# Raw scores leave PSUM on ScalarE, and the key norm is folded with a small product and applied two slots later

## The chip, the cores and the metric

The kernel runs on one core of a Trainium2 chip. Five engines work side by side, each through its own list of instructions in order: TensorE (PE, with its weight loads PEld), VectorE (DVE), ScalarE (ACT), GpSimd (POOL) and SyncE (SP). TensorE writes to PSUM only; ScalarE and VectorE read PSUM and SBUF. Transfers are issued from SP's and ACT's lists. The metric is the time of one execution on the device in microseconds (us). Before the change it is 2100.78 us, the median of two runs (2096.07 and 2105.5).

## What is computed

Eight batches of 64 tokens of width 512 pass one layer: a cross and self attention of 8 groups of heads, a second attention with a learned sparse mask, and a feed-forward network. The change lies in the cross attention of the tokens to 1601 context rows per batch. Cut to that part:

```python
# per batch b and group g (8 groups, two query heads each: 128 query rows), d = 128
kx, vx = split(cond @ w_kv_x.T)              # keys and values of the 1601 context rows
kx = _ln(kx, kxln_w, kxln_b)                 # layer norm of each key over its 128 features
qx = _ln(fp8_linear(ln_out, wqx), qxln_w, qxln_b)
scores = einsum('bsghd,btgd->bghst', qx, kx) / sqrt(128)
p = softmax(scores)                          # over the 1601 rows
out = einsum('bghst,btgd->bsghd', p, vx)
```

The mean of a key is taken out of the weights ahead of time. The scale, one over the root of the key's variance plus 1e-5, is one number for each key and group. Since it is common to all features of a key, it can multiply the finished scores: score = (query times unscaled key) times scale(key), plus a constant of the query.

## The kernel before, in words

The cross attention is cut into 16 passes (class `Cross`): 8 batches times 2 halves of 4 groups. A pass goes over 13 tiles of 128 context rows (`TT`). The tiles are grouped in six chunks (`CHUNKS`), five of two tiles (256 rows) and a last one of three (321 rows). Keys of a chunk are made two groups at a time (one at a time in part of the last chunk); scores are made, normed and turned into probabilities by chunk; probabilities are transposed and used tile by tile.

One loop over g issues the work of all passes as a pipeline: in step (slot) g, tile g is read and split, tile g-2 (`KEYS`) becomes keys, and so on. There are 208 slots and a tail. Keys, queries and probabilities are split into a high and a low part, and each product of two split numbers takes three products on TensorE.

- `keys` (L569 to L599): 12 products per group into a PSUM bank (L585). ACT squares the bank (L592) and copies it, scaled, to the high part `kthi` (L593); DVE transposes the squares in blocks of 32 (L595), takes the low part `ktlo` (L596) and adds up the squares (L597). The result `kms` holds, on each of 128 partitions, sums over parts of the features: feature sums still lie on four blocks of 32 partitions.
- `norm` (L601 to L617), at the end of the slot in which a chunk's last keys are made: DVE copies the four blocks beside each other (L609, four copies on 32 partitions), adds them for each group (L611, four reductions), POOL raises to the power -0.5 (L613), DVE transposes (L615), and SP writes the row of scales to `keyd` in device memory (L617).
- `spread` (L619 to L623), two slots later: an ACT-issued transfer reads the row back into a tile `S`, broadcast to all 128 partitions, 512 KB.
- `scores` (L625 to L649), three slots after the keys (`SCORES` 5 against `KEYS` 2): TensorE makes the scores into one of three PSUM banks of a pool (`mainp`), which keys, scores and transposed probabilities share. DVE multiplies each group's scores by the scales in `S`, writes the product over them in `S` and keeps the maximum (L646). For the last chunk, DVE also copies the query's constant (L649).
- `maxima` and `exps`: after a pass's last chunk, the row maximum, and exponentials on ACT in place in `S` (L662). `S` has eight buffers.
- `probs_t`, `weigh`: 15 or more slots later the probabilities are transposed by TensorE (L674), split by ACT and DVE (L684, L685), and multiplied with the context (L737 to L739).

Beside the passes run generators (`bgA`, `bgB`, `bgC`) at a set pace: projections, the self attention, the output products (L440), the second attention (`attn`, L804 on) and the preparation of the feed-forward weights. The feed-forward network itself ends the program.

A planner fixes each engine's order of instructions ahead of time. It gives preference to what stands earlier in the program, among what its own clock holds to be ready. `tc.issue_after(x)` only puts an instruction behind x on its engine. At run time an engine that waits holds up all that stands behind it, and a transfer issued from ACT's list waits there for its data.

Of the kernel before, what the change touches and what calls it, by code (L numbers as in the profile page):

```python
# [11 lines left out]
F32 = mybir.dt.float32  # L12
F32R = mybir.dt.float32r
# [8 lines left out]
P = 128  # L22
# [19 lines left out]
LAG = 20  # L42
KEYS, SPREAD, SCORES = 2, 4, 5
ALL = 10 ** 6
# [17 lines left out]
def tile_perceiver(ctx: ExitStack, tc: tile.TileContext, t: dict):  # L62
# [168 lines left out]
    for h in range(2):  # L231
        V.tensor_copy(fold[h * S:(h + 1) * S], ident[h * S:(h + 1) * S, h * S:(h + 1) * S])
    spread = [ctile([P, 32], F32, f"spread{i}") for i in range(2)]
    parts = [ctile([32, HG * NRM, 5], F32, f"parts{i}") for i in range(2)]
    for x, y in zip(spread, parts):
        V.memset(x, 0.0)
        V.memset(y, EPS)
    mhalf = ctile([P, NRM], F32, "mhalf")
# [63 lines left out]
    def projection(v_, blocks, js, first=None):  # L302
# [17 lines left out]
        for nb in blocks:  # L320
# [17 lines left out]
            for i0 in range(0, len(js), 2):  # L338
# [14 lines left out]
                if v_ == "v":  # L353
# [5 lines left out]
                    continue  # L359
                st = sm("hst", 24)  # L360
                ag = sm("hag", 8)
# [168 lines left out]
    class Cross:  # L530


        def __init__(self, b, half):
            self.b, self.half = b, half
            self.raw = None
            self.S = {}
            self.kt = {}
            self.ct = {}
            self.ms = {}
            self.qb = sm("cqb", HG, bufs=2)  # L540
# [60 lines left out]
        def norm(self, ci):  # L601

            cw = sum(TT[tt][1] for tt in CHUNKS[ci])
            nj = (cw + 31) // 32
            ms = self.ms.pop(ci)
            x = parts[ci % 2]
            r = spread[ci % 2]
            for i in range(4):
                V.tensor_copy(x[:, :HG * nj, i], ms[i * 32:(i + 1) * 32, :HG * nj])  # L609
            for g in range(HG):  # L610
                V.tensor_reduce(r[g * 32:(g + 1) * 32, :nj], x[:, g * nj:(g + 1) * nj], AX.X, ALU.add)  # L611
            with tc.issue_after(low[0].ins):
                GP.tensor_tensor(r[:, :nj], r[:, :nj], mhalf[:, :nj], ALU.pow)  # L613
            rt = sm("krt", 32, bufs=2)
            V.transpose(rt, r)  # L615
            rd = keyd[(self.b + self.half * NB) % 2][ci]
            nc.sync.dma_start(rd.rearrange("g (x a) -> (g x) a", a=32), rt)  # L617

        def spread(self, ci):  # L619

            cw = sum(TT[tt][1] for tt in CHUNKS[ci])
            self.S[ci] = mp.tile([P, HG, KTW], F32, tag="S", name=nm("S"), bufs=SB)
            nc.scalar.dma_start(self.S[ci][:, :, :cw], keyd[(self.b + self.half * NB) % 2][ci][:, :cw].partition_broadcast(P))  # L623

        def scores(self, ci):  # L625
            chunk = CHUNKS[ci]
            cw = sum(TT[tt][1] for tt in chunk)
            hi, lo = self.kt.pop(ci)
            N = cw + (cw & 1)
            if N > cw:  # L630

                for x, y in ((hi, kbhi), (lo, kblo)):
                    gp_copy(x[:, :, cw:N], y.bitcast(F32).unsqueeze(2))
            sc = self.S[ci]
            per = 512 // N
            for g0 in range(0, HG, per):
                bank = mainp("s")
                gs = range(g0, g0 + per)

                for k, (a, x) in enumerate(((self.qhi, hi), (self.qlo, hi), (self.qhi, lo))):  # L640
                    for i, g in enumerate(gs):
                        PE.matmul(bank[:, i * N:(i + 1) * N], lhsT=a[:, g * P:(g + 1) * P], rhs=x[:, g, :N],  # L642
                                  start=k == 0 and i == 0, stop=k == 2, skip_group_check=True)
                for i, g in enumerate(gs):
                    ps = bank[:, i * N:(i + 1) * N]
                    V.tensor_tensor_reduce(sc[:, g, :cw], ps[:, :cw], sc[:, g, :cw], 1.0, -3.0e38,  # L646
                                           ALU.mult, ALU.max, self.mx[:, g * NCH + ci:g * NCH + ci + 1])
                    if N > cw:
                        V.tensor_copy(self.qb[:, g:g + 1], ps[:, cw:N])  # L649

        def maxima(self):

            top = sm("ctop", HG)
            V.tensor_reduce(top, v3(self.mx, HG), AX.X, ALU.max)
            V.tensor_tensor(top, top, self.qb, ALU.add)
            self.nmx = sm("cnm", HG)
            V.tensor_tensor(self.nmx, self.qb, top, ALU.subtract)  # L657

# [38 lines left out]
        def context(self, tt):  # L697
            t0, n = TT[tt]
            if tt == len(TT) - 1:
# [3 lines left out]
                chi = mp.tile([P, 512], F32R, tag="chi", name=nm("chi"), bufs=2)  # L703
                clo = mp.tile([P, 512], F32R, tag="clot", name=nm("clot"), bufs=1)
                A.copy(chi, raw)
# [98 lines left out]
    def attn(j, x, o=0, n=P, kept=False, L=bgl):  # L804
# [92 lines left out]
        else:  # L897
# [3 lines left out]
            V.tensor_scalar(sim[:n], ps[:n, :S], at["b3"][:n], None, ALU.add)  # L901
        for b in range(nb):
            r = slice(b * S, (b + 1) * S)
            GP.affine_select(out=sim[r], in_=sim[r], compare_op=ALU.not_equal, fill=0.0, base=0,
                             pattern=[[-1, S]], channel_multiplier=1)
        yield
# [16 lines left out]
        for k0, k1 in ((0, 4), (4, KSEL)):  # L923
            w = (k1 - k0) * P
            sel = fa()
            GP.memset(sel, 0.0)
            for b in range(nb):
# [78 lines left out]
    def ffn_rows(pairs, kind):  # L1006

        if kind == 0:
            z2 = ph.tile([P, 2, NIC, 256], F32R, tag="ws", name=nm("z2"), bufs=1)
            rows = ph.tile([P, 2, 512], F32, tag="cats", name=nm("fx"), bufs=1)  # L1010
            ac["ffn_b2"] = bcast_row(mp.tile([P, 512], F32, tag="sq", name=nm("b2"), bufs=1), t["ffn_b2"])
        else:
# [192 lines left out]
    for g in range(NA + LAG + 3):  # L1205
# [26 lines left out]
        if 0 <= g - SPREAD < NA and LAST[kN]:  # L1232
            with tc.issue_after(turn[0].ins):
                work[nN].spread(JOBS[kN][0])
        if 0 <= g - SCORES < NA:
            nS, kS = divmod(g - SCORES, NT)
            ci = CHUNK_OF[kS]
            w = work[nS]
            if kS == CHUNKS[ci][-1]:
                if ci == 0:  # L1240
                    w.queries()
                w.scores(ci)
                if ci == NCH - 1:
                    w.maxima()
                    w.exps(0, 0, 2)
        if g == LAG - 4:
# [18 lines left out]
        if g == TERNARY_AT:  # L1265
            bgB.add(ternary("ffn_w1", w1t), ternary("ffn_w2", w2t))
        if 0 <= g - SCORES - 1 < NA and (g - SCORES - 1) % NT == NT - 1:
            work[(g - SCORES - 1) // NT].exps(0, 2, 4)
        e = g - LAG
# [113 lines left out]
```

## Time and profile before

| quantity | value |
|---|---|
| median of the runs | 2100.78 us (2096.07 and 2105.5) |
| the profiled execution | 2105.96 us, of which the span of its instructions is 2104.2 us |
| PE busy | 1903.1 us, 90% of the span |
| DVE busy | 1501.6 us, 71% |
| ACT busy | 1097.7 us, 52% |
| POOL busy | 557.7 us, 27% |
| transfers | 406.33 MB, 193 GB/s on the mean |
| granted TensorE clock | 0.96 on the mean |

A group of instructions is written as line, engine, operation, output <- inputs, size and count, then busy time and mean duration, then the idle time of the engine just ahead of them with what ended it. A line of the waits gives who waited for whom, the total in us, how often, and the longest. TensorE's products overlap each other, so the mean duration of one (0.28 us for 256 columns) is longer than the distance between two starts.

### The profile page before, as it was taken

Reading aid. Unit: us, or ns where it says so; the run is one execution under the profiler, and the core shown is the slowest. Engines: PE = TensorE matmul, PEld = TensorE weight load, DVE = VectorE, ACT = ScalarE, POOL = GpSimd, SP = SyncE. Lnnn points to the kernel's source line nnn. Section 1 sums busy time; section 2 is a strip of 40 time slices with the busy share of each in tenths; the row PEclk is TensorE's granted clock in tenths of the full one; section 3 lists DMA queues with packets and bytes.
Section 4 is the critical chain, followed back from the end, with each engine's and each line's share of the span. In section 5 each row is a group of like instructions: output and inputs, shape, how many; then the busy total and the mean of one; then the engine's idle time right before and its main releaser. Section 6 shows DMA issues by size and latency. Waiting matters only on the chain.

```text
span 2104.2 us, 36122 instructions
## 1 busy us (share of the span) xinstructions
PE 1903.1 (90%) x11989; PEld 1657.8 (79%) x11989; DVE 1501.6 (71%) x4339; ACT 1097.7 (52%) x2628; POOL 557.7 (27%) x487
## 2 busy tenths in 40 slices
PE   5679998999999899899999999899999999846997
PEld 5568897898988889798888889798887787524766
DVE  7768787878888868977776766576667667534565
ACT  6446654665665555654454444444456545413554
POOL 4332323322323223222222222222223222000132
PEclk9889999999999999999999999999999999958999
DMA  6546565577666567567868777676784665521424
GB/s 197 158 124 186 170 181 159 175 224 241 198 173 189 176 206 229 172 209 235 301 224 260 253 249 244 227 257 209 229 292 128 180 195 165 181 97 62 145 76 150
DMA packets 361036, 406.33 MB, mean 193 GB/s; under 512 B 45696, under 2 KB 255744, under 8 KB 360848
## 3 DMA queue, kind: packets, MB, share of 16 engines
q1 hardware_dynamic: 310160, 351.54, 51.8%
q10 hardware_dynamic: 50688, 52.47, 10.1%
q8 instruction: 95, 1.56, 0.3%
q14 instruction: 93, 0.76, 0.1%
HBM read 336.40 MB, written 67.26 MB: 192 GB/s over the span
## 4 chain that ended last, share of the span: by engine, by line
PE 59%; DMA 18%; DVE 12%; ACT 4%; issue 4%; POOL 1%; SPq 1%; ACTq 0%; POOLq 0%; DVEq 0%
PE kx L585 20%; PE acc L738 5%; PE acc L737 5%; PE acc L739 5%; DMA S<-keyd 5%; DMA ws<-wpd 5%; PE s L642 4%; PE pt L674 3%; PE pp L440 3%; PE pj L349 3%; PE xo L758 2%; PE p L866 2%; DMA keyd<-krt 1%; DMA wv<-in_wkv 1%; DVE S L646 1%
## 5 line engine op out<-in xcount | busy, mean ns | idle before, releaser
L567 POOL TENSOR_TENSOR cTlo<-cTr,cThi 128x512 fp32r<-128x512 f32 (+1 forms) x208 | 247.5, 1191 | 732.3 <-ACT cThi L566 668.0
L738 PE MATMUL acc<-plo,chi 128*128 128x512 f32 x768 | 308.0, 403 | 0.9 <-DVE plo L685 0.9
L739 PE MATMUL acc<-phi,clo 128*128 128x512 f32 x768 | 302.6, 397 | 0.0
L592 ACT ACTIVATE ksq<-kx 128x512 f32<-128x512 f32 (+1 forms) x224 | 123.9, 553 | 340.9 <-PE kx L585 312.0
L585 PE MATMUL kx<-cThi,wkhi 128*128 128x256 f32 (+1 forms) x1536 | 271.6, 297 | 29.7 <-ACT cThi L566 11.6
L585 PEld LDWEIGHTS kx<-cThi,wkhi 128*128 128x128 f32 x1536 | 226.2, 193 | 52.3 <-ACT cThi L566 13.8
L595 DVE STREAM_TRANSPOSE ksqt<-ksq 128x512 f32<-128x512 f32 (+1 forms) x224 | 147.3, 658 | 165.3 <-ACT ksq L592 164.4
L585 PE MATMUL kx<-cTlo,wkhi 128*128 128x256 f32 (+1 forms) x1536 | 261.6, 290 | 0.6 <-POOL cTlo L567 0.6
L585 PE MATMUL kx<-cThi,wklo 128*128 128x256 f32 (+1 forms) x1536 | 259.8, 290 | 0.0
L613 POOL TENSOR_TENSOR spread<-spread,mhalf 128x8 f32<-128x8 f32 x96 | 171.6, 1787 | 325.9 <-DVE spread L611 310.8
L737 PE MATMUL acc<-phi,chi 128*128 128x512 f32 x768 | 247.9, 409 | 2.0 <-ACT phi L684 1.7
L646 DVE CUSTOM_DVE_ANT_0 S<-s,S 128x256 f32<-128x256 f32 (+1 forms) x384 | 152.6, 429 | 105.3 <-DMA S<-keyd 80.3
L585 PEld LDWEIGHTS kx<-cTlo,wkhi 128*128 128x128 f32 x1536 | 220.9, 191 | 5.8 <-issue 2.4
L585 PEld LDWEIGHTS kx<-cThi,wklo 128*128 128x128 f32 x1536 | 221.6, 193 | 4.4 <-issue 4.1
L662 ACT ACTIVATE S<-S,cnm 128x256 f32<-128x256 f32 (+1 forms) x384 | 197.7, 524 | 45.6 <-DVE cnm L657 45.5
L714 ACT CAST chi<-cr 128x512 fp32r<-128x512 f32 x192 | 119.6, 623 | 117.5 <-PE acc L738 64.5
L738 PEld LDWEIGHTS acc<-plo,chi 128*128 128x128 f32 x768 | 147.0, 192 | 27.0 <-issue 2.0
L739 PEld LDWEIGHTS acc<-phi,clo 128*128 128x128 f32 x768 | 145.7, 190 | 26.7 <-issue 1.6
L737 PEld LDWEIGHTS acc<-phi,chi 128*128 128x128 f32 x768 | 139.4, 192 | 26.4 <-ACT phi L684 3.5
L674 PE MATMUL pt<-ident,S 128*128 128x128 f32 (+1 forms) x832 | 138.7, 277 | 20.3 <-ACT S L662 10.3
L685 DVE TENSOR_TENSOR plo<-pt,phi 128x512 fp32r<-128x512 f32 x192 | 130.9, 682 | 30.4 <-ACT phi L684 29.5
L596 DVE SCALAR_TENSOR_TENSOR ktlo<-kx,cols,kthi 128x512 fp32r<-128x512 f32 (+1 forms) x224 | 147.8, 660 | 0.0
(347 smaller groups left out, 3696.4 us busy)
## 6 DMA issues: line engine op xcount, KB each, us to landing
cTr<-in_ctxT SPq DMA_DIRECT2D x192, 256.0 KB
cr<-in_ctx SPq DMA_DIRECT2D x192, 256.0 KB
ws<-wpd SPq DMA_DIRECT2D x88, 512.0 KB
S<-keyd ACTq DMA_DIRECT2D x80, 512.0 KB
clod<-clo SPq DMA_DIRECT2D x96, 256.0 KB
clo<-clod SPq DMA_DIRECT2D x96, 256.0 KB
wv<-in_wkv SPq DMA_DIRECT2D x64, 256.0 KB
tern<-in_ffn_w SPq DMA_DIRECT2D x64, 256.0 KB
```

The source lines that it names most:

```text
L567: low[0] = GP.tensor_tensor(clo[:, :, o:o + n], raw[:, :, :n], chi[:, :, o:o + n].bitcast(F32), ALU.subtract)
L585: PE.matmul(ps[:, i * N:(i + 1) * N], lhsT=st[:, ic, g * P:(g + 1) * P], rhs=mv[:, ic, :N], start=k == 0, stop=k == 11)
L595: V.transpose(sqt[:, :ng * W], sq[:, :ng * W])
L596: V.scalar_tensor_tensor(lo[:, g0:g1, :N], v3(ps[:, :ng * N], ng), hw["kx"], hi[:, g0:g1, :N].bitcast(F32), ALU.mult, ALU.subtract)
L613: GP.tensor_tensor(r[:, :nj], r[:, :nj], mhalf[:, :nj], ALU.pow)
L646: V.tensor_tensor_reduce(sc[:, g, :cw], ps[:, :cw], sc[:, g, :cw], 1.0, -3.0e38, ALU.mult, ALU.max, self.mx[:, g * NCH + ci:g * NCH + ci + 1])
L662: A.activation(self.S[ci][:, g, :cw], self.S[ci][:, g, :cw], AF.Exp, bias=self.nmx[:, g:g + 1], accum_out=self.su[:, g * NCH + ci:g * NCH ...
L674: PE.transpose(pt[:n, g * P:(g + 1) * P], self.S[ci][:, g, o:o + n], ident)
L685: V.tensor_tensor(lo[:n], pt[:n], hi[:n].bitcast(F32), ALU.subtract)
L737: PE.matmul(self.U[ic], lhsT=chi[:n, s], rhs=phi[:n], start=tt == 0, stop=False)
L738: PE.matmul(self.U[ic], lhsT=chi[:n, s], rhs=plo[:n], start=False, stop=False)
L739: PE.matmul(self.U[ic], lhsT=clo[:n, s], rhs=phi[:n], start=False, stop=False)
```

## The change

ScalarE copies the raw scores of a whole bank out of PSUM into `S`. VectorE multiplies them in place in a new method `tops`, two slots later, with a tile `row` that the broadcast transfer now fills; `row` has one buffer. The constant of the query is read from `S` and no longer copied. `scores` moves from three slots behind the keys to one slot behind, and takes `norm` with it: `norm` no longer gathers the four blocks of partitions on VectorE but multiplies `kms` with a constant matrix `over` on TensorE (which adds the four blocks and spreads the sums over them), adds 1e-5 and keeps each partition's own group with the mask `quad` in one VectorE instruction, and adds over the groups in a second. The product goes into one more tile of the three-bank pool, behind the last product of the scores. The queries are loaded and split at a pass's first tile. Beside this: the diagonal of the mask's scores is set to zero by a multiplication on VectorE in place of a GpSimd select, a tile is cleared on VectorE in place of GpSimd, the narrow feed-forward weights of the first part load into the two buffers `cTr` in place of the three `raw`, and some buffers are shared or fewer.

```diff
-KEYS, SPREAD, SCORES = 2, 4, 5
+KEYS, SCORES, SPREAD, TOPS = 2, 3, 4, 5
...
+    quad = ctile([P, HG], F32, "quad")
+    for h in range(HG):
+        V.tensor_reduce(quad[:, h:h + 1], ident[:, h * 32:(h + 1) * 32], AX.X, ALU.add)
+    over = ctile([P, P], F32, "over")
+    for h in range(HG):
+        V.tensor_reduce(over[:, h * 32:(h + 1) * 32], ident.rearrange("p (q a) -> p a q", q=HG), AX.X, ALU.add)
...
-    parts = [ctile([32, HG * NRM, 5], F32, f"parts{i}") for i in range(2)]
...
+    off = ctile([P, S], F32, "off")
+    V.tensor_scalar(off, fold, -1.0, 1.0, ALU.mult, ALU.add)
...
-                st = sm("hst", 24)
+                st = sm("hst", 24, bufs=2)
...
         def norm(self, ci):
...
             ms = self.ms.pop(ci)
-            x = parts[ci % 2]
+            z = mainp("kz")
+            with tc.issue_after(self.sm.ins):
+                PE.matmul(z[:, :HG * nj], lhsT=over, rhs=ms[:, :HG * nj], start=True, stop=True)
+            own = sm("kown", HG * NRM, bufs=1)
+            V.scalar_tensor_tensor(v3(own[:, :HG * nj], HG), v3(z[:, :HG * nj], HG), EPS, quad.unsqueeze(2).to_broadcast([P, HG, nj]), ALU.add, ALU.mult)
+            v = sm("kxv", NRM, bufs=2)
+            V.tensor_reduce(v[:, :nj], own[:, :HG * nj].rearrange("p (g j) -> p j g", g=HG), AX.X, ALU.add)
             r = spread[ci % 2]
-            for i in range(4):
-                V.tensor_copy(x[:, :HG * nj, i], ms[i * 32:(i + 1) * 32, :HG * nj])
-            for g in range(HG):
-                V.tensor_reduce(r[g * 32:(g + 1) * 32, :nj], x[:, g * nj:(g + 1) * nj], AX.X, ALU.add)
             with tc.issue_after(low[0].ins):
-                GP.tensor_tensor(r[:, :nj], r[:, :nj], mhalf[:, :nj], ALU.pow)
+                GP.tensor_tensor(r[:, :nj], v[:, :nj], mhalf[:, :nj], ALU.pow)
...
         def spread(self, ci):
...
-            self.S[ci] = mp.tile([P, HG, KTW], F32, tag="S", name=nm("S"), bufs=SB)
-            nc.scalar.dma_start(self.S[ci][:, :, :cw], keyd[(self.b + self.half * NB) % 2][ci][:, :cw].partition_broadcast(P))
+            self.row = mp.tile([P, HG, KTW], F32, tag="row", name=nm("row"), bufs=1)
+            nc.scalar.dma_start(self.row[:, :, :cw], keyd[(self.b + self.half * NB) % 2][ci][:, :cw].partition_broadcast(P))
...
         def scores(self, ci):
...
-            sc = self.S[ci]
+            sc = self.S[ci] = mp.tile([P, HG, KTW], F32, tag="S", name=nm("S"), bufs=SB)
...
-                for i, g in enumerate(gs):
-                    ps = bank[:, i * N:(i + 1) * N]
-                    V.tensor_tensor_reduce(sc[:, g, :cw], ps[:, :cw], sc[:, g, :cw], 1.0, -3.0e38,
-                                           ALU.mult, ALU.max, self.mx[:, g * NCH + ci:g * NCH + ci + 1])
-                    if N > cw:
-                        V.tensor_copy(self.qb[:, g:g + 1], ps[:, cw:N])
+                A.copy(sc[:, g0:g0 + per, :N], v3(bank[:, :per * N], per))
+
+        def tops(self, ci):
+
+            cw = sum(TT[tt][1] for tt in CHUNKS[ci])
+            sc = self.S[ci]
+            for g in range(HG):
+                V.tensor_tensor_reduce(sc[:, g, :cw], sc[:, g, :cw], self.row[:, g, :cw], 1.0, -3.0e38,
+                                       ALU.mult, ALU.max, self.mx[:, g * NCH + ci:g * NCH + ci + 1])
...
-                clo = mp.tile([P, 512], F32R, tag="clot", name=nm("clot"), bufs=1)
+                clo = mp.tile([P, 512], F32R, tag="clo", name=nm("clot"), bufs=2)
...
-        for b in range(nb):
-            r = slice(b * S, (b + 1) * S)
-            GP.affine_select(out=sim[r], in_=sim[r], compare_op=ALU.not_equal, fill=0.0, base=0,
-                             pattern=[[-1, S]], channel_multiplier=1)
+        V.tensor_tensor(sim[:n], sim[:n], off[:n], ALU.mult)
...
-            GP.memset(sel, 0.0)
+            V.memset(sel, 0.0)
...
-            tag, bufs = ("kthi", "ktlo")[k] if kind else "raw", 2 if kind else 3
+            tag, bufs = ("kthi", "ktlo")[k] if kind else "cTr", 2
...
+        nN, kN = divmod(g - TOPS, NT)
+        if 0 <= g - TOPS < NA and LAST[kN]:
+            ci = JOBS[kN][0]
+            w = work[nN]
+            w.tops(ci)
+            if ci == NCH - 1:
+                w.maxima()
+                w.exps(0, 0, 2)
         if 0 <= g - SCORES < NA:
             nS, kS = divmod(g - SCORES, NT)
-            ci = CHUNK_OF[kS]
-            w = work[nS]
-            if kS == CHUNKS[ci][-1]:
-                if ci == 0:
-                    w.queries()
+            if LAST[kS]:
+                ci = JOBS[kS][0]
+                w = work[nS]
                 w.scores(ci)
-                if ci == NCH - 1:
-                    w.maxima()
-                    w.exps(0, 0, 2)
+                w.norm(ci)
+            elif kS == 0:
+                work[nS].queries()
...
-        if 0 <= gK < NA and LAST[kK]:
-            work[nK].norm(JOBS[kK][0])
```

More of the change, by code (lines that the diff above doesn't have):

```diff
@@ L232, in tile_perceiver @@
         V.tensor_copy(fold[h * S:(h + 1) * S], ident[h * S:(h + 1) * S, h * S:(h + 1) * S])
+    quad = ctile([P, HG], F32, "quad")
[4 more added lines that the diff above has]
+        V.tensor_reduce(over[:, h * 32:(h + 1) * 32], ident.rearrange("p (q a) -> p a q", q=HG), AX.X, ALU.add)
     spread = [ctile([P, 32], F32, f"spread{i}") for i in range(2)]
-    parts = [ctile([32, HG * NRM, 5], F32, f"parts{i}") for i in range(2)]
-    for x, y in zip(spread, parts):
+    for x in spread:
         V.memset(x, 0.0)
-        V.memset(y, EPS)
+    off = ctile([P, S], F32, "off")
+    V.tensor_scalar(off, fold, -1.0, 1.0, ALU.mult, ALU.add)
     mhalf = ctile([P, NRM], F32, "mhalf")
@@ L539, in __init__ @@
             self.ms = {}
-            self.qb = sm("cqb", HG, bufs=2)
             self.pp = {}
@@ L641, in scores @@
                     for i, g in enumerate(gs):
-                        PE.matmul(bank[:, i * N:(i + 1) * N], lhsT=a[:, g * P:(g + 1) * P], rhs=x[:, g, :N],
+                        self.sm = PE.matmul(bank[:, i * N:(i + 1) * N], lhsT=a[:, g * P:(g + 1) * P], rhs=x[:, g, :N],
                                   start=k == 0 and i == 0, stop=k == 2, skip_group_check=True)
-                for i, g in enumerate(gs):
-                    ps = bank[:, i * N:(i + 1) * N]
-                    V.tensor_tensor_reduce(sc[:, g, :cw], ps[:, :cw], sc[:, g, :cw], 1.0, -3.0e38,
-                                           ALU.mult, ALU.max, self.mx[:, g * NCH + ci:g * NCH + ci + 1])
-                    if N > cw:
-                        V.tensor_copy(self.qb[:, g:g + 1], ps[:, cw:N])
+                A.copy(sc[:, g0:g0 + per, :N], v3(bank[:, :per * N], per))
[5 more added lines that the diff above has]
+                                       ALU.mult, ALU.max, self.mx[:, g * NCH + ci:g * NCH + ci + 1])
         def maxima(self):
@@ L654, in maxima @@
             V.tensor_reduce(top, v3(self.mx, HG), AX.X, ALU.max)
-            V.tensor_tensor(top, top, self.qb, ALU.add)
+            qb = self.S[NCH - 1][:, :, SC - TT[CHUNKS[-1][0]][0]]
+            V.tensor_tensor(top, top, qb, ALU.add)
             self.nmx = sm("cnm", HG)
-            V.tensor_tensor(self.nmx, self.qb, top, ALU.subtract)
+            V.tensor_tensor(self.nmx, qb, top, ALU.subtract)
         def exps(self, ci, g0=0, g1=HG):
@@ L1010, in ffn_rows @@
             rows = ph.tile([P, 2, 512], F32, tag="cats", name=nm("fx"), bufs=1)
-            ac["ffn_b2"] = bcast_row(mp.tile([P, 512], F32, tag="sq", name=nm("b2"), bufs=1), t["ffn_b2"])
+            ac["ffn_b2"] = bcast_row(mp.tile([P, 512], F32, tag="row", name=nm("b2"), bufs=1), t["ffn_b2"])
         else:
@@ L1266, in tile_perceiver @@
             bgB.add(ternary("ffn_w1", w1t), ternary("ffn_w2", w2t))
-        if 0 <= g - SCORES - 1 < NA and (g - SCORES - 1) % NT == NT - 1:
-            work[(g - SCORES - 1) // NT].exps(0, 2, 4)
+        if 0 <= g - TOPS - 1 < NA and (g - TOPS - 1) % NT == NT - 1:
+            work[(g - TOPS - 1) // NT].exps(0, 2, 4)
         e = g - LAG
```

## The prediction

> **What bounds the kernel now.** I began with busy time by stretches of the span: after the first 200 us TensorE works nearly without rest, VectorE and ScalarE do not (columns: us, then busy time and count of PE, PEld, DVE, ACT, POOL, then granted clock, share and rate of the transfers).
>
> ```profile
> 0.00:200.00 200.00, 141.32 (x942) 132.07 (x943) 154.52 (x484) 103.61 (x243) 72.10 (x70) 0.91 0.57 165
> 400.00:600.00 200.00, 194.70 (x1322) 177.93 (x1320) 166.35 (x511) 127.22 (x320) 64.00 (x53) 1.00 0.69 207
> 1200.00:1400.00 200.00, 189.96 (x1211) 169.68 (x1210) 135.10 (x379) 90.96 (x227) 51.13 (x43) 0.98 0.72 230
> ```
>
> So from 200 to 1800 us a change is worth what it takes from or gives to TensorE's list, plus what it takes from TensorE's waits. I next added up those waits, gap by gap. From 200 to 1800 us they are 72.6 us: 38.8 ended by DVE, 20.1 by transfers, 13.7 by ACT. In the first 200 us they are 58.6 (27.8 DVE, 30.3 ACT), after 1800 us 64.8 (35.4 DVE). DVE is the engine that TensorE waits for most. Then the groups by line, to see which DVE work it is:
>
> ```profile
> L585 PE MATMUL kx<-cThi,wkhi 128*128 128x256 f32 (+1 forms) x1536 | 271.6, 297 | 29.7 <-ACT cThi L566 11.6 <-DVE cmx L646 5.3 <-DVE cqb L649 5.2
> ...
> L646 DVE CUSTOM_DVE_ANT_0 S<-s,S 128x256 f32<-128x256 f32 (+1 forms) x384 | 152.6, 429 | 105.3 <-DMA S<-keyd 80.3 <-PE s L642 21.3 <-PE out L965 1.6
> ...
> L642 PE MATMUL s<-kthi,qxhi 128*128 128x256 f32 (+1 forms) x384 | 92.6, 308 | 22.8 <-DVE cmx L646 8.9 <-DVE cqb L649 5.1 <-ACT cThi L566 5.1
> L609 DVE COPY parts<-kms 32x32 f32<-32x32 f32 (+1 forms) x384 | 79.0, 206 | 4.5
> ...
> L611 DVE TENSOR_REDUCE spread<-parts 32x8 f32<-32x40 f32 (+1 forms) x384 | 71.0, 185 | 4.7
> ```
>
> The reader sees two things. The multiplication of the scores (L646) keeps DVE idle for 80.3 us until the row of scales lands, and all the while a PSUM bank with scores is held: products of keys and scores wait for it. And the fold of the norm is 768 instructions of some 0.2 us, 150.0 us of DVE. Last, the chain of the work that ended last shows what a row costs in latency when it is on the path:
>
> ```profile
> 1240.24 2.11 POOL spread L613
> 1242.61 2.90 DMA keyd<-krt
> 1245.52 11.34 DMA S<-keyd
> ```
>
> Elsewhere in that chain the row's read takes 5.1 to 9 us and its write 2.4 to 4.2.
>
> **The change, part by part.** The sum is made against the profiled execution, 2105.96 us (span 2104.2). It lies 5.2 us (0.25%) above the median 2100.78; I add the same difference to the median.
>
> *Bank released by ACT.* The products that wait for L646 or L649 now wait for an ACT copy. The groups give 5.3 + 5.2 (keys), 8.9 + 5.1 (scores), and 2.7 for the transposes L674: 27.2 us that go. What is late next is ACT. It gains per pass ten copies of 512 columns and four of 322. The copy of 512 columns out of PSUM (L684) takes 0.595 us, L592 on 322 columns 0.443 (by form): 16 x (10 x 0.595 + 4 x 0.443) = 124 us, so ACT goes from 1097.7 to 1222 us, 58%. It lies beside TensorE's work. ACT now makes TensorE wait 58.7 us in the whole span; with 11% more load I give back 6 us. Bounds: nothing, and all 27 if the copy queues as L646 did. Sum -21.
>
> *The fold on TensorE.* 96 products, plain float32. The trace has no product `over` by `kms`. The nearest row is L758, also float32: 256 products have 512 records, two each, and in the chain ten of its records take 1.13 us, 0.11 each. That makes 96 x 2 x 0.11 = 21 us. TensorE is some 5% idle in the middle stretch, so I take +20. Below: 11, if a record of 32 columns costs half of one of 128. Above: 48, at 0.5 us each, if it also stands waiting for `kms`, which DVE finishes (L597, 0.625 us) after `ktlo`, on which the scores just ahead of it depend. A product that waits holds up every product behind it.
>
> *VectorE.* Off go 79.0 + 71.0 of the fold and 9.7 of L649. On come 192 instructions (one out of PSUM, one reduction, 128x32); the nearest rows are L609 and L611 at 0.2 us: 38 us. The 384 multiplications stay and read SBUF; no row shows that form, so I keep 0.43 us, with 0.3 (the distance of two starts is 0.35) and 0.5 as ends: +-40 us of DVE. In all DVE goes from 1501.6 to about 1380 us, 66%. TensorE's other waits for DVE between 200 and 1800 us are 38.8 less 18.0 for L646 and L649, so 21 us. Queueing at 66% in place of 71% is about a fifth shorter (0.66/0.34 = 1.94 against 0.71/0.29 = 2.45): -5. In the first 200 us DVE is 77% busy and the fold of some ten chunks is 16 us of it; TensorE is short of work there, so half of the 12 us saved goes through: -6. Bounds of both together: 0 and -30.
>
> The Trainium skill (VectorE: DVE Perf Modes, Rules for kernel authors) speaks against the detour: on a matmul's output accept the rate out of PSUM, or copy to SBUF first if many operations follow. Here one follows. The same page's table of fixed costs (The TRN2 errata) puts an SBUF source 62 cycles of VectorE below a PSUM source. By that, an estimate, the multiplications would lose 384 x 65 ns = 25 us; by the rule alone the copy would be 124 us for nothing. The rows decide otherwise than the rule only because what it buys is a free bank, not a cheaper operation.
>
> *The row.* Before, from the end of a chunk's last `kms` (medians over 78 chunks, from the starts of the lines) the fold ends at 3.9 us, the write is issued at 6.7, the read at 11.2, the score products start at 16.2 and the multiplication at 19.2. After it, the scores must come first (one slot of 8.7 us behind the keys at most), the fold takes 1 in place of 2.8 us, the multiplication keeps its slot. The row then lands about when it did, with a spread of several us either way. I take 0 for DVE's wait of 80.3 us and treat the rest as a rival. The read is issued from ACT's list; behind it stand the squares, `kthi`, and the copies of probabilities, for which TensorE waits. ACT now idles 27.8 us there, ten times. `row` has one buffer, so the read also waits for the chunk before it to be multiplied, a slot earlier. Value 0, bounds -10 and +30.
>
> *Queries.* They are split on POOL three slots earlier, behind the last scores of the pass before. POOL waited 19.5 us for them in seven cases, TensorE for POOL's `cTlo` 0.6 us in the whole span; POOL is 27% busy, that hides it. Without that cover it is 15 waits of up to 5.7 us.
>
> *The last stretch.* The select and ten clears of 0.52 us leave POOL, where they wait 51.0 + 24.6 us for transfers; DVE gets some 6 us of 154 in 305. DVE waited for that select 7.0 us in all, so the wait moves rather than goes: 0. Weights in two own buffers in place of three shared: ACT and POOL wait 20.5 us for them now; 0. Bounds for both -10 and +10. Shared and fewer buffers elsewhere: 0, no wait names them.
>
> Sum: -21 + 20 - 5 - 6 = -12 us on paper. TensorE also loses time in gaps under 0.15 us that no wait names: between 200 and 1800 us products start about 60 us later in total than at their usual distances. Fewer banks held and a less loaded DVE should take a sixth of it, -10. So -22: 2084 in the profile, **2079** against the median, 1% faster and inside the band.
>
> **The rivals.**
>
> *DVE was the real limit* (faster). For: 102 us of TensorE's idle time end with DVE, and the startup is not bound by TensorE. Against: the fold pays 20 us on the bound engine, and the transfers' 20 us stay. If two thirds of the 102 go, 68, and half of the 60 small ones, 30, against 20 + 6 given back: -72, so 2029 against the median; the case begins at -42, 2059, and its middle is 2044.
>
> *The row comes late* (slower). One mechanism: scores, fold, power, write, read and multiplication now hang one behind the other, within two slots (17.3 us). The parts add up to 0.7 (scores) + 1.5 (fold with its hand-overs) + 1.8 + 0.5 + 2.9 + 6.9 = 14.3 us without any queue. If the planner puts the multiplication 4 us ahead of the landing, DVE stands 96 x 4 = 384 us, and since 101.6 us of waits at L646 cost TensorE 27 us, TensorE loses about a quarter: +100, so 2179. It outweighs the gain from 2.5 us per chunk on (+64 - 22 = +42, 2143). Against: the bank is no longer held meanwhile, so less than a quarter may come through.
>
> *The waits only change their name.* ACT and the fold take back what DVE gave: 2085 to 2110. It is inside the band too.
>
> **How the numbers follow.** A change under 2% (42 us) is about what a measurement of this kernel can't tell from none. Forecast and the third rival together 0.46 (2059 to 2143), faster rival 0.32, late row 0.22. The range reaches into both: 2030 to 2150, which leaves about a tenth out at each end.
>
> **What would show it.** Right: L646 and L649 gone from what keys and scores wait for; the fold's product with two records of 0.11 us distance; DVE near 1380 and ACT near 1220 us; waits of the multiplication for `row` near 80 us. Wrong: those waits above 240 us, scores waiting for `ktlo`, the fold's product waiting for `kms`, or ACT idle over 60 us for `keyd`.

## The result

The changed kernel takes 2222.74 us, the median of two runs (2222.6 and 2222.89), against 2100.78 before: a ratio of 1.0581, with a 95% interval of 1.0478 to 1.0683. The forecast was 2079 us, in a range of 2030 to 2150. The profiled span is 2221.0 us against 2104.2, so 116.8 us more.

The busy times of the changed kernel's page come first (busy us, share of the span, count).

```profile
span 2221.0 us, 35931 instructions
PE 1954.8 (88%) x12181; PEld 1695.3 (76%) x12181; DVE 1389.1 (63%) x3721; ACT 1201.7 (54%) x2852; POOL 549.5 (25%) x469
```

VectorE lost 112.5 us of work and ScalarE took on 104, nearly as worked out. Yet every engine's share but ScalarE's fell, TensorE's from 90% to 88%: something stands more. The same stretches as before, in the same columns (us, then busy time and count of PE, PEld, DVE, ACT, POOL, then granted clock, share and rate of the transfers):

```profile
0.00:200.00 200.00, 142.17 (x953) 131.84 (x954) 136.90 (x420) 111.05 (x258) 71.84 (x68) 0.91 0.56 160
400.00:600.00 200.00, 183.82 (x1202) 165.84 (x1202) 132.04 (x378) 122.95 (x307) 53.32 (x47) 0.97 0.63 195
1200.00:1400.00 200.00, 183.86 (x1186) 163.38 (x1184) 115.57 (x292) 97.13 (x233) 48.38 (x40) 0.99 0.73 232
```

The start is as it was. The loss is in the pipeline of passes: TensorE finishes 1202 products in the second stretch where it finished 1322. The first keys of the last pass begin at 1819 us instead of 1690. These 129 us are the whole loss; what follows gives 12 back. The groups by line name the place (busy us, mean ns of one, then idle time of the engine just ahead and what ended it).

```profile
L590 PE MATMUL kx<-cThi,wkhi 128*128 128x256 f32 (+1 forms) x1536 | 281.1, 304 | 26.7 <-DVE ktlo L601 9.5 <-DVE plo L696 6.9 <-DVE kown L615 6.2
...
L658 DVE CUSTOM_DVE_ANT_0 S<-S,row 128x256 f32<-128x256 f32 (+1 forms) x384 | 163.0, 473 | 295.2 <-DMA row<-keyd 295.2
...
L649 PE MATMUL s<-kthi,qxhi 128*128 128x256 f32 (+1 forms) x384 | 93.4, 311 | 64.6 <-DVE ktlo L601 50.9 <-POOL kthi L521 7.5 <-DVE plo L696 4.6
...
L613 PE MATMUL kz<-kms,over 128*128 128x32 f32 x192 | 33.9, 260 | 12.8 <-DVE plo L696 4.7 <-DVE kms L602 4.3 <-ACT S L651 3.3
```

The multiplication (now L658) keeps VectorE idle for 295.2 us until the row of scales lands; before it was 80.3. It no longer holds a PSUM bank meanwhile: the waits for `cmx` and `cqb` are gone from the lines of keys and scores, as predicted. But the scores (L649) now wait 50.9 us for `ktlo`, the low part of the keys, where the same line waited 22.8 us in all before. The two waits, as us in total, times, and the longest:

```profile
DVE S L658 <- DMA row<-keyd: 295.2, 91, 10.0
...
PE s L649 <- DVE ktlo L601: 64.5, 32, 5.9
```

The second takes all three kinds of score products together. VectorE stands in 91 of 96 chunks. Why that reaches `ktlo` is seen in VectorE's own list. The timeline of VectorE in one slot (start us, us, operation; in brackets the idle time just before and what ended it):

```profile
1179.58 0.42 DVE L658 CUSTOM_DVE_ANT_0 S<-S,row 128x256 f32<-128x256 f32 x1 [5.53 <-DMA row<-keyd]
...
1180.28 0.42 DVE L658 CUSTOM_DVE_ANT_0 S<-S,row 128x256 f32<-128x256 f32 x1
1180.63 0.08 DVE L658 DVE_READ_ACCUMULATOR2_ANT cmx<- 128x1 f32 x1
1180.63 0.75 DVE L601 SCALAR_TENSOR_TENSOR ktlo<-kx,cols,kthi 128x512 fp32r<-128x512 f32 x1
```

VectorE stands 5.53 us for the row, and `ktlo` of a newer tile of keys waits behind. TensorE, at the same time, waits for that `ktlo` before its next scores:

```profile
1181.43 0.51 PE L649 MATMUL s<-kthi,qxhi 128*128 128x256 f32 x2 [2.84 <-DVE ktlo L601]
```

On the chain of the work that ended last the row's read is now the largest piece: the page puts it at 15% of the span, where the same read was 5% before. One link of that chain:

```profile
1030.93 0.43 ACT kthi L598
...
1031.40 5.64 DMA row<-keyd
...
1038.34 0.34 DVE S L658
```

The following table adds up TensorE's idle gaps of over 0.15 us, as the prediction did, by what ended them.

| stretch | before | after |
|---|---|---|
| 0 to 200 us | 58.6 | 57.5 |
| 200 to 1800 us | 72.6 (38.8 by DVE) | 135.6 (106.3 by DVE) |
| after 1800 us | 64.8 | 67.7 |

Idle gaps account for 65 of the 117 us. The other 52 are busy time (1954.8 less 1903.1). The median distance between two products of keys in a row stayed at 0.12 us, but the mean rose from 0.129 to 0.132, and the mean granted clock fell from 0.960 to 0.952. If all of TensorE's work scaled with that clock, it would be 0.008/0.96 of 1903 = 16 us, an estimate. Some 14 us are the fold's own products (worked out below). The rest would be short delays that lie under the modelled ends of the products; no record shows them.

### The profile page after: what moved, and what is told of

The parts are those of the page before. It is cut to its first block, busy times and chain, and to the rows that moved or that the text cites. A ratio compares the mean times of both kernels' runs of the same rounds, so it can differ in the third digit from the quotient of the medians.

```text
span 2221.0 us, 35931 instructions
## 1 busy us (share of the span) xinstructions
PE 1954.8 (88%) x12181; PEld 1695.3 (76%) x12181; DVE 1389.1 (63%) x3721; ACT 1201.7 (54%) x2852; POOL 549.5 (25%) x469
## 4 chain that ended last, share of the span: by engine, by line
PE 42%; DMA 26%; DVE 16%; ACT 7%; issue 6%; POOL 2%; SPq 1%; ACTq 0%; DVEq 0%; POOLq 0%
DMA row<-keyd 15%; PE kx L590 13%; PE acc L749 4%; PE acc L750 4%; PE acc L748 3%; DVE S L658 3%; PE s L649 3%; DMA ws<-wpd 2%; PE pt L685 2%; DMA keyd<-krt 2%; PE xo L769 2%; PE p L877 2%; PE pj L355 1%; DVE ktlo L601 1%; DVE ksqt L600 1%
## 5 line engine op out<-in xcount | busy, mean ns | idle before, releaser
L572 POOL TENSOR_TENSOR cTlo<-cTr,cThi 128x512 fp32r<-128x512 f32 (+1 forms) x208 | 244.3, 1175 | 620.6 <-ACT cThi L571 557.8
L658 DVE CUSTOM_DVE_ANT_0 S<-S,row 128x256 f32<-128x256 f32 (+1 forms) x384 | 163.0, 473 | 295.2 <-DMA row<-keyd 295.2
L590 PE MATMUL kx<-cThi,wkhi 128*128 128x256 f32 (+1 forms) x1536 | 281.1, 304 | 26.7 <-DVE ktlo L601 9.5
L620 POOL TENSOR_TENSOR spread<-kxv,mhalf 128x8 f32<-128x8 f32 x96 | 171.2, 1783 | 471.8 <-DVE kxv L617 367.8
L651 ACT COPY S<-s 128x512 f32<-128x512 f32 (+1 forms) x224 | 119.2, 546 | 162.3 <-PE s L649 153.0
L685 PE MATMUL pt<-ident,S 128*128 128x128 f32 (+1 forms) x832 | 135.6, 277 | 29.2 <-ACT S L673 21.4
L649 PE MATMUL s<-kthi,qxhi 128*128 128x256 f32 (+1 forms) x384 | 93.4, 311 | 64.6 <-DVE ktlo L601 50.9
```

The costliest lines, as they stand in the source:

```text
L572: low[0] = GP.tensor_tensor(clo[:, :, o:o + n], raw[:, :, :n], chi[:, :, o:o + n].bitcast(F32), ALU.subtract)
L590: PE.matmul(ps[:, i * N:(i + 1) * N], lhsT=st[:, ic, g * P:(g + 1) * P], rhs=mv[:, ic, :N], start=k == 0, stop=k == 11)
L620: GP.tensor_tensor(r[:, :nj], v[:, :nj], mhalf[:, :nj], ALU.pow)
L649: self.sm = PE.matmul(bank[:, i * N:(i + 1) * N], lhsT=a[:, g * P:(g + 1) * P], rhs=x[:, g, :N], start=k == 0 and i == 0, stop=k == 2, ski ...
L658: V.tensor_tensor_reduce(sc[:, g, :cw], sc[:, g, :cw], self.row[:, g, :cw], 1.0, -3.0e38, ALU.mult, ALU.max, self.mx[:, g * NCH + ci:g * N ...
L685: PE.transpose(pt[:n, g * P:(g + 1) * P], self.S[ci][:, g, o:o + n], ident)
```

## The experiments

**Theory.** The planner puts the multiplication too early in VectorE's list: VectorE reaches it before the row has landed, stands, and `ktlo` comes late to scores that follow the keys by only one slot. The trace gives the sizes. Between the end of the fold and the multiplication stood a median of 25 instructions of VectorE before the change (reads of the accumulator left out), and 12 stand there now. From the read's issue on ScalarE's list, VectorE reached the multiplication after 6.56 us before the change (median) and reaches it after 3.43 us now. The row, where VectorE stands for it, lands 6.93 us after issue before (41 of 96 chunks, so the late ones) and 6.21 us now (91 of 96). So nothing shows a slower transfer; the reader comes 3.1 us sooner, and VectorE stands 3.24 us per stand.

**Rivals.** The early scores themselves do the harm (they wait for `ktlo` whatever VectorE does). The fold's product on TensorE does it. The copies load ScalarE.

The kernel before ran beside each set of runs: it took 2119.57 us beside the constant row, the scores later, the fold alone and the first of the two delays; 2110.19 beside the other single executions; 2098.57 (median of 25, from 2089.19 to 2112.72) beside the kernels that ran several times. Ratios of single executions are to these times and have no interval. Ratios with an interval come from executions side by side and differ from the ratio of the two medians by up to 0.0014.

### The multiplication without the row

The multiplication takes a constant one in place of the row. The scales are thus left out of the scores; the fold, the power, the write and the read all stay.

```diff
-                V.tensor_tensor_reduce(sc[:, g, :cw], sc[:, g, :cw], self.row[:, g, :cw], 1.0, -3.0e38,
+                V.tensor_tensor_reduce(sc[:, g, :cw], sc[:, g, :cw], ones[:, :1].to_broadcast([P, cw]), 1.0, -3.0e38,
```

> The multiplication takes a constant one in place of the row of scales, so it waits for no transfer; the fold, the power, the write and the broadcast read all stay. The scales are left out of the scores in this run. If VectorE's stand for the row (295 us before the multiplication) is the cause, the time falls from 2223 to between 2080 and 2120 us, and the scores' wait for ktlo (64 us on TensorE) falls below 25 us with it. If the cause is that the scores stand one slot behind the keys, whatever the row does, the time stays above 2180 us and TensorE's wait for ktlo stays above 50 us. If it is the fold's product on TensorE, the time stays above 2180 us without the wait for ktlo.

It took 2047.51 us, a ratio of 0.966, less than any theory expected. The wait of the scores, and the busy times of the page:

```profile
PE s L649 <- DVE ktlo L601: 5.8, 6, 1.8
```

```profile
PE 1895.6 (93%) x12181; PEld 1664.4 (81%) x12181; DVE 1396.7 (68%) x3721; ACT 1202.5 (59%) x2852; POOL 558.9 (27%) x469
```

With the same number of instructions on every engine, the wait for `ktlo` falls from 64.5 to 5.8 us, and TensorE's busy time falls by 59 us too. (The granted clock rises from 0.952 to 0.972; if all of TensorE's work scaled with it, that would be 40 of the 59, an estimate.) With the 295 us of standing on VectorE go 175 us by the two times, or 193 by the two ratios (1.0581 and 0.966, of 2100.78): some six tenths of it. The early scores, the fold's product and the copies are all still there: none of them by itself is the loss.

The edit does one thing more. With no row to wait for, the planner moves the multiplication ahead of the fold in all 96 chunks (a median of 10.5 us before the read's issue). So wait and place change together here, and the price of the standing is only as good as that. The kernel before was not run without its row, so the 0.966 does not say what the change would gain.

### The multiplication later in VectorE's list

Two edits delay it without changing what it does. In the first the block that calls `tops` stands behind the slot's keys, and is put behind their last sum.

```diff
+            with tc.issue_after(pin[0].ins):
+                w.tops(ci)
```

> Nothing is left out. The multiplication is put behind the sums of squares (kms) of the slot's keys on VectorE, so that about 25 more VectorE instructions stand between the fold and it (median 38 in place of 13 in the planned order). If the place of the multiplication ahead of the row's landing is the cause, VectorE's wait for the row falls from 295 to under 80 us and the time to between 2085 and 2130 us. If the scores' nearness to ktlo is the cause by itself, the wait for the row falls too, but the time stays above 2180 us.

In the second it stays in its place in the program and is put behind the low part of the probabilities last split (L696 of the changed kernel; here `plow` holds that instruction).

```diff
-            w.tops(ci)
+            with tc.issue_after((plow[0] or pin[0]).ins):
+                w.tops(ci)
```

> A small dose of the delay of e2: the multiplication is put behind the slot's low part of the probabilities (plo), so the planned order has a median of 18 VectorE instructions between the fold and it, against 13 after the change and 38 in e2. Nothing is left out. If the time goes with the stand for the row, some 5 instructions of 0.3 to 0.7 us take 1.5 to 3 of the 3 us per chunk: the wait for the row falls to between 100 and 230 us, the time to between 2140 and 2200 us. If only the move to another slot counts, the time stays at 2223.

The first took 2105.65 us (ratio 0.9934), the second 2084.66 (0.9879). The waits of the first:

```profile
PE pt L685 <- ACT S L673: 45.6, 11, 9.1
...
DVE S L658 <- DMA row<-keyd: 12.4, 8, 2.5
...
PE s L649 <- DVE ktlo L601: 8.2, 5, 3.1
```

The waits of the second, whose lines lie one further down:

```profile
DVE S L659 <- DMA row<-keyd: 125.5, 50, 6.1
...
PE s L650 <- DVE ktlo L602: 9.3, 4, 4.0
```

In VectorE's list a median of 12 instructions (reads of the accumulator left out) stand between the end of the fold and the multiplication in the changed kernel, 17 in the second edit and 34 in the first. Five more instructions, and VectorE reaches the multiplication 6.03 us after the read's issue in place of 3.43. That takes off more than half of the standing and nearly all of the scores' waiting. The wait fell as expected, but the time fell far below the 2140 to 2200 us expected: 125.5 us of standing in pieces of 2.5 us do little harm, so the harm does not grow in proportion to the standing. The first edit takes off almost all of the standing and has the higher ratio. There the last chunk's scores are multiplied so late that the exponentials are late, and the transposes of the probabilities (L685) wait 45.6 us for them. So I expected that an early last chunk would bring those back:

```diff
-        if 0 <= g - TOPS < NA and LAST[kN]:
+        if 0 <= g - TOPS < NA and kN == NT - 1:
...
+        if 0 <= g - TOPS < NA and LAST[kN] and kN < NT - 1:
+            ci = JOBS[kN][0]
+            w = work[nN]
+            with tc.issue_after(pin[0].ins):
+                w.tops(ci)
```

> e2, but a pass's last chunk is multiplied at its place in the changed kernel, since e2 let the transposes of probabilities wait 45.6 us on TensorE for the exponentials that follow the last chunk. That wait should fall under 15 us, for about 16 stands of VectorE of some 3 us more (48 us, a quarter of it on TensorE): 2070 to 2105 us. If that wait has another cause, it stays and the time does not fall.

It took 2111.81 us (1.0008): a miss. The transposes' wait fell to 20.4 us and the time did not. VectorE's standing rose to 53.8 us, as was to be expected, so what the transposes' wait costs stays open. Each edit makes the planner lay out all lists anew, and 25 executions of the kernel before alone spread over 23.5 us. I read no difference of that size between single executions.

### The scores one slot later

Here the scores go back one slot, to two behind the keys, and the fold stays where it was. The multiplication is left early.

```diff
-KEYS, SCORES, SPREAD, TOPS = 2, 3, 4, 5
+KEYS, NORM, SCORES, SPREAD, TOPS = 2, 3, 4, 4, 5
...
-            with tc.issue_after(self.sm.ins):
-                PE.matmul(z[:, :HG * nj], lhsT=over, rhs=ms[:, :HG * nj], start=True, stop=True)
+            PE.matmul(z[:, :HG * nj], lhsT=over, rhs=ms[:, :HG * nj], start=True, stop=True)
...
+        if 0 <= g - NORM < NA and LAST[(g - NORM) % NT]:
+            work[(g - NORM) // NT].norm(JOBS[(g - NORM) % NT][0])
...
-                w.norm(ci)
```

> The scores stand two slots behind the keys in place of one; the fold stays one slot behind, without the order behind the scores. The multiplication keeps its place. If the row is the cause, VectorE still stands 200 to 330 us for it, and the time gains only what TensorE lost at ktlo: 2150 to 2210 us. If the nearness of the scores to ktlo is the cause, TensorE's wait for ktlo falls below 20 us and the time to between 2090 and 2140 us.

It took 2267.75 us (1.0699), slower than anything expected. Its waits:

```profile
DVE S L658 <- DMA row<-keyd: 305.3, 85, 9.9
...
PE acc L748 <- ACT phi L695: 49.6, 23, 7.5
...
PE kz L613 <- DVE kms L602: 39.6, 23, 5.4
...
PE acc L748 <- DVE ut L756: 20.9, 7, 4.5
...
PE s L649 <- DVE ktlo L601: 4.1, 5, 0.9
```

The scores' wait for `ktlo` is gone, and the loss is not. VectorE stands as long as before (305.3), and TensorE now waits for whatever else is behind the standing: the probabilities, the key sums, the outputs. So the early scores are only where the delay came through. The two delays leave the scores early, take off the standing (nearly all or more than half of it), and the loss is gone. Together with this run, that shows the standing to be the cause, and `ktlo` its nearest customer. With both edits together (scores later and the first of the two delays), the standing should go and the scores be safe:

```diff
-KEYS, SCORES, SPREAD, TOPS = 2, 3, 4, 5
+KEYS, NORM, SCORES, SPREAD, TOPS = 2, 3, 4, 4, 5
...
+            with tc.issue_after(pin[0].ins):
+                w.tops(ci)
```

> e2 and e3 together: the scores two slots behind the keys and the multiplication behind the slot's kms. If the 45 us that e3 lost against the changed kernel also came from VectorE standing for the row, they go with the stand: 2095 to 2130 us and a wait for the row under 60 us. If they belong to the scores' later place itself, 2140 us or more.

It took 2072.1 us (0.982), with 4.6 us of standing, better than expected. Beside the smaller delay and two parts of the change, it then ran several times.

### Several executions of each

> The kernel of e4 again, timed in rounds beside the kernel before. If its look was no chance: a ratio of 0.975 to 0.99 to the kernel before, clear of one, so that the changed kernel with two places moved beats both.

The kernel with both edits takes 2068.23 us (four runs, 2057.03 to 2073.3), a ratio of 0.9844 to before, with an interval of 0.9796 to 0.9891. Its page and waits:

```profile
PE 1909.4 (92%) x12181; PEld 1671.9 (81%) x12181; DVE 1395.9 (68%) x3721; ACT 1201.1 (58%) x2852; POOL 544.5 (26%) x469
```

```profile
PE pt L685 <- ACT S L673: 18.7, 16, 6.2
...
DVE S L658 <- DMA row<-keyd: 5.7, 3, 2.9
```

It is faster than both kernels, and keeps the copies, the fold on TensorE and the multiplication in place.

> The kernel of e12 again, timed in rounds: a ratio of 0.98 to 0.995 to the kernel before. A place that leaves VectorE 125 us of standing would then cost little against one that leaves 5 us.

The five more instructions alone give 2086.96 us, 0.9931 (0.9906 to 0.9956): the loss is gone, and a little more.

The fold on TensorE, alone in the kernel before (scores, multiplication and copies as they were):

```diff
-            for i in range(4):
-                V.tensor_copy(x[:, :HG * nj, i], ms[i * 32:(i + 1) * 32, :HG * nj])
-            for g in range(HG):
-                V.tensor_reduce(r[g * 32:(g + 1) * 32, :nj], x[:, g * nj:(g + 1) * nj], AX.X, ALU.add)
+            z = mainp("kz")
+            PE.matmul(z[:, :HG * nj], lhsT=over, rhs=ms[:, :HG * nj], start=True, stop=True)
+            own = sm("kown", HG * NRM, bufs=1)
...
+            V.tensor_reduce(v[:, :nj], own[:, :HG * nj].rearrange("p (g j) -> p j g", g=HG), AX.X, ALU.add)
```

> The kernel before, with only the fold changed to the product on TensorE and two VectorE instructions; scores, lags and the broadcast into S as before. From the rows after: two records of 0.11 us and what surrounds them make 21 us on TensorE at most, VectorE loses some 112 us. Both theories: within 2085 to 2130 us, so the fold is not the cause. If the fold's product is the cause, it is above 2170 us.

> The kernel of e5 again, timed in rounds: the fold alone on TensorE at a ratio of 0.98 to 0.995 to the kernel before. If TensorE's bound made the fold a loss, as the prediction's term of +20 us had it, the ratio is above 1.

A single execution took 2089.08 us; the median of ten is 2087.34, a ratio of 0.9951 (0.9929 to 0.9973). In the single one the fold's product stands for the key sums, and the multiplication waits less than before the change:

```profile
DVE S L651 <- DMA S<-keyd: 44.9, 19, 6.7
PE kz L611 <- DVE kms L601: 43.4, 20, 9.9
```

I then moved the fold to the end of the slot, behind the weighing, to take that stand away:

```diff
-        if 0 <= gK < NA and LAST[kK]:
-            work[nK].norm(JOBS[kK][0])
...
+        if 0 <= gK < NA and LAST[kK]:
+            work[nK].norm(JOBS[kK][0])
         if g == NA + FFN_AT:
```

> e5 with the call of the norm moved to the end of the slot, behind the products with the context and the background work, since in e5 TensorE stood 43.4 us before the fold's product for kms. If that stand is lost time, it falls below 15 us and the time to between 2050 and 2080 us; if it only took idle time, 2085 to 2100 us.

It took 2092.45 us (0.9916). The stand is 31.6 us, so the planner put the product only a little later, and nothing was gained. Whether the fold would give more without its stand stays open.

Last, the rest of the change without the fold: the kernel with both edits, with the old fold on VectorE (its parts in one buffer) and the select back on GpSimd. The copies, the late multiplication, the early queries and the changed buffers stay.

```diff
-                PE.matmul(z[:, :HG * nj], lhsT=over, rhs=ms[:, :HG * nj], start=True, stop=True)
...
+            for i in range(4):
+                V.tensor_copy(x[:, :HG * nj, i], ms[i * 32:(i + 1) * 32, :HG * nj])
+            for g in range(HG):
+                V.tensor_reduce(r[g * 32:(g + 1) * 32, :nj], x[:, g * nj:(g + 1) * nj], AX.X, ALU.add)
...
-        V.tensor_tensor(sim[:n], sim[:n], off[:n], ALU.mult)
+        for b in range(nb):
+            r = slice(b * S, (b + 1) * S)
+            GP.affine_select(out=sim[r], in_=sim[r], compare_op=ALU.not_equal, fill=0.0, base=0,
+                             pattern=[[-1, S]], channel_multiplier=1)
```

> e4 with the old fold on VectorE (eight instructions a chunk, one buffer for the parts) and the old select on GpSimd: what is left of the change is the copy of raw scores by ScalarE and the later multiplication, at places where VectorE does not stand. If the fold carries the gain of e4, the ratio to the kernel before is 0.995 to 1.01. If the copy carries it, below 0.985.

It took 2112.12 us, a ratio of 1.0054 (1.0026 to 1.0081). The row does not matter here (VectorE stands 7.4 us for it), and yet the detour through ScalarE gains nothing. The wait for the row in the whole span, then the longest of TensorE's waits from 200 to 1800 us:

```profile
DVE S L650 <- DMA row<-keyd: 7.4, 2, 7.2
```

```profile
PE pp L440 <- DMA ws<-wpd: 29.0, 21, 6.8
PE tr L381 <- ACT fa L376: 19.9, 9, 3.2
PE kx L584 <- ACT cThi L565: 17.7, 19, 1.3
```

The 18.0 us that keys, scores and transposes waited for L646 and L649 in that stretch are gone; TensorE now waits for ScalarE instead, 37.6 us in the two lines shown and 53.4 in all, where its waits for ScalarE came to 13.7 before the change. The copies alone do not make these waits: the changed kernel, the run without the row and the smaller delay have the same copies, and there the sum is 14.5, 8.8 and 14.9 us. So the 0.5% is the price in this layout, with the multiplication far back, and not of the copies by themselves.

## Why the prediction was wrong

**The step that failed is the row.** "The multiplication keeps its slot. The row then lands about when it did" gave 0 for VectorE's wait of 80.3 us, with bounds of -10 and +30 us of time. Measured: 295.2 us of standing, which cost some 180 us by the run without the row. The row does land about when it did; what failed is the step from the slot to the wait. Counted from the last key sum, over all 96 chunks (medians before, then now): fold done 3.7 and 4.9 us, write issued 6.7 and 8.4, read issued 11.2 and 11.1, multiplication started 19.0 and 18.3. So the read starts when it did. (The fold is not done sooner, as forecast, but 1.2 us later.) The slot was kept, but it does not fix the place in VectorE's list: 12 instructions stand between the fold and the multiplication in place of 25, and VectorE reaches it 3.1 us sooner after the read's issue.

What I took for the row's slack before the change was the score products: the multiplication had to wait for them on TensorE, and they started 3.0 us before it. Once the scores are made early, nothing but the row holds the multiplication back, and the planner orders it by its own idea of the landing, which the chip shows to be some 3 us too soon. That the planner had placed it by the row is shown by the run without the row, where the multiplication moves ahead of the fold. That the late scores had held it before is argued: no run puts the scores back to their old slot under the copies. The fold is not what moved it: alone in the kernel before, it leaves 44.9 us of standing.

**The late-row rival named the mechanism and underpriced it.** It supposed 4 us of standing in every chunk, 384 us in all; 3.24 us in 91 chunks came. It priced a quarter: from 215 us more of standing (295.2 less 80.3), 54 us. TensorE's idle time ended by VectorE in the middle stretch did rise by 67.5 us, nearly a third. But the whole time rose by 116.8, because the price left out TensorE's busy time, which rose by 52 (some 14 of it the fold's). Its counter-argument, that less comes through once no bank is held, was wrong: the same wait then held up `ktlo`, on which scores one slot behind the keys depend. I had listed "scores waiting for `ktlo`" as a sign and put no price on it. The other sign, ScalarE idle for the row's write, did not come: 10.0 us in five cases, against 27.8 in ten before. I gave this rival 0.22.

**Bank released by ACT, -21.** The waits for L646 and L649 went as said, and ScalarE came to 1201.7 us against the 1222 worked out. The give-back of 6 us is mis-sized: in the changed kernel ScalarE makes TensorE wait 54.4 us where it was 58.7, in the run without the new fold 80.9. There, with the row out of the way and the old fold in place, the rest of the change costs 0.5% (1.0026 to 1.0081). The Trainium skill (VectorE: DVE Perf Modes, Rules for kernel authors), to accept the rate out of PSUM where one operation follows, agrees with that ratio; I had set it aside because a bank was to be bought.

**The fold, +20, and VectorE, -5 and -6.** Together +9; alone in the kernel before they measure -10 us (-15 to -6), from 0.9951 of 2098.57. The mis-sized term is the fold's +20. Two records per product came, as predicted, but the second starts 0.04 us after the first and the next product 0.11 us after that, so 0.15 us per fold or 14 us. In the changed kernel it stands 12.8 us, so the upper bound of 48 was not reached. VectorE came to 1389.1 us for 1380. In the first 200 us TensorE's idle time fell by 1 us, not 6, in the changed kernel, and by 9 with the fold alone. There, in the fastest of the ten executions, the idle time is 49.3, 83.6 and 30.9 us in the three stretches of the table (58.6, 72.6 and 64.8 before): the gain lies ahead of the middle stretch and behind it. That VectorE's shorter list pays for those 14 us and more is argued, not shown.

**The multiplication out of SBUF.** I kept 0.43 us between 0.3 and 0.5. On 256 columns the median is 420 ns after and 419 before, at median distances of 0.346 and 0.345 us. The 25 us that I worked out from the table of the Trainium skill (VectorE: DVE Perf Modes, The TRN2 errata) for a source out of SBUF did not appear; the measurement decides. The mean rose, from 418 to 466 ns, for a reason that I had not seen: 25 of the 384 multiplications take 0.6 to 1.5 us. Each of them starts while GpSimd works on `cTlo` (L572) and ends 0.28 to 0.35 us after GpSimd does:

```profile
449.94 1.20 POOL L572 TENSOR_TENSOR cTlo<-cTr,cThi 128x512 fp32r<-128x512 f32 x1 [2.14 <-ACT cThi L571]
...
450.37 1.05 DVE L658 CUSTOM_DVE_ANT_0 S<-S,row 128x256 f32<-128x256 f32 x1 [2.10 <-DMA row<-keyd]
```

With one source in PSUM, none of the 384 did before, though 12 started under the same GpSimd operation. It is a small part of the loss (the line is busy 163.0 us in place of 152.6), and the best version has more of it (53).

**Queries and last stretch, 0.** POOL's wait for the last scores grew from 19.5 to 78.9 us (14 times), and none of TensorE's waits names the queries' split. After 1800 us TensorE idles 67.7 us in place of 64.8. Both hold. **Small gaps, -10:** in the changed kernel they grew; whether they would shrink without the standing can be read only from the run without the row, whose mean distance of two key products is 0.129 us, as before. So 0.

**What stays open.** Whether the early multiplication with later scores is really another 1% slower than the changed kernel: its 1.0699 is one execution against one, and the changed kernel's interval reaches to 1.0683. TensorE's waits for what is behind the standing are named above, but not why they would cost more. And how the 1.6% of the best version splits: the fold alone gives 0.5%, the rest without it loses 0.5%, so the two together gain more than their sum. In it TensorE idles 153.1 us in gaps over 0.15 us, against 196.0 before. That VectorE's lighter list needs a free bank to pay is a guess that no run here tests.

## What to carry to other kernels

When a dependency is moved away from an instruction, ask what had been timing that instruction: here, it seems, the late scores had kept a reader behind its transfer without anyone having meant it. On an engine that works in order, an instruction with a transfer as its last input belongs behind other work by a written order, with at least the measured time from issue to landing between them (6.2 us here, where 3.4 were left), and what it would hold up is to be listed before the change. Five instructions put in between turned +5.8% into -0.7%.

## What was not expected of the hardware

- TensorE's busy time moved with VectorE's standing, not only its idle time: 1895.6 us without the row, 1909.4 in the best version and 1954.8 in the changed kernel, with the same 12181 products. The mean granted clock moved along. Among single executions on one chip it was 0.943 with 305 us of standing, 0.950 in the kernel before, 0.963 with the first delay and 0.972 without the row. The traces do not separate the clock from short delays, nor what is cause and what is effect.
- The read of a row of scales into all 128 partitions took a median of 6.21 us from issue to landing where VectorE stood for it (5.2 to 7.7 for the middle eighty per cent).
- A VectorE multiplication with both sources in SBUF that starts under a GpSimd subtraction of 128x512 takes up to 1.46 us in place of 0.42, and ends 0.28 us or a little more after it. With one source in PSUM it takes 0.42 under the same subtraction.
- Small plain float32 products start 0.04 and 0.11 us apart, well under the 0.26 us that one is recorded to last.
